# A Mamba block and a quantised feed-forward net on one core: three of eight C products on GpSimd, at other places, and another slack for the sums

## Chip, cores and metric

The kernel runs on one core of a Trainium2 chip. The metric is the device time of one launch in microseconds; the median of nine runs stands for the kernel. The engines are called by the profile's names: PE (matrix multiply), PEld (its weight load), DVE (vector), ACT (activation), POOL (GpSimd), SP (the queue that issues the DMAs).

## What is computed

Eight images of 384 channels and 1024 positions go through a Mamba-like block and an MLP, and then (five of the eight) through a feed-forward net with binarised weights and quantised activations. All is float32. The part that the change touches is the selective scan:

```
xz = t @ in_proj_w.T; xm, z = split(xz)
xc = silu(conv(xm, 3 taps))
dt, Bm, Cm = split(xc @ x_proj_w.T)
dt = softplus(dt @ dt_proj_w.T + dt_proj_b)
dA  = exp(einsum('bld,dn->bldn', dt, A))
dBu = einsum('bld,bln->bldn', dt * xc, Bm)
def step(hst, inp):
    dA_t, dBu_t, C_t = inp
    hst = dA_t * hst + dBu_t
    return hst, einsum('bdn,bn->bd', hst, C_t)
y = scan(step) + xc * D
y = y * silu(z)
t = y @ out_proj_w.T
t = gelu(t @ mlp_w1.T + mlp_b1) @ mlp_w2.T + mlp_b2
```

There are 768 inner channels d and 16 states n.

## The kernel before

**Stages.** `write_down` goes over the eight images b (called batches in the code). `s1` normalises, projects, convolves and makes dt, dt times xc, z and the rows of B and C, which go to DRAM. `s2` is the scan. `s3` is the output projection and the MLP. `ffn` is the quantised net for the first five images; `binarise` prepares its weights once, beside image 0. The matmuls of s1, s3 and ffn pass through `matmuls` (L444).

**The scan.** `scan` handles one image in 12 units. A unit has eight tiles: two tiles i (0 and 1) for each of four quads q (four states each). A tile is 128 partitions (32 channels times four states) by 1024 positions. In the first and the last image the work is done in halves of the positions, and a tile holds two pieces of 512. For one tile, `scan_tile` writes down these steps:

- ACT: da = exp(dt times A), into a PSUM buffer (L460; ring "da" of two buffers);
- POOL: u = dtx times B, into an SBUF buffer (L798; ring "u" of nine buffers);
- DVE: the scan over positions (L802), written into da, or into u where the tile is "on POOL";
- the product with C: on DVE, u = da times C (L819), or on POOL, u = u times C (L816);
- in the first half of the first and the last image also a copy of the last column as state, by ACT (L813) or POOL (L810).

`on_pool(i, q)` says which tiles have their product with C on POOL: now i = 1 with q = 1 and q = 3, two of eight.

When two quads are done (BATCH = 2: four tiles), one PE step `sums` adds the four states of all four tiles into the PSUM tile py (L729, 16 recorded matmuls); with it their four u buffers come free. After the unit's second step of sums DVE adds xc times D (L759), and POOL multiplies by z (L769, in the last image L765).

**What sets the order.** Every operation is first written down with an engine, a cost and its dependencies (`Plan.add`). `Plan.run` is a list scheduler: it runs a model of the five engines, picks the next operation for each by lane and image, and emits the instructions in that order. Each engine then works through its queue in order. Operations of lane 0 are the scan; DVE and POOL prefer operations of other lanes that are ready, PE prefers the sums (lane -1). What an operation uses of a ring is free again when its last user has ended in the model. SLACK is a time that is added to the end of the sums' inputs:

```
op.slack = SLACK if self.prio[0] < 0 else 0.0
```

and, for each operation `n` that follows an operation,

```
n.ready = max(n.ready, end + n.slack + (0.0 if n.engine == e != "SP" else SIGNAL))
```

(the attribute is the follower's own), so the sums are not planned before SLACK has passed after their last input. Where the model finds PE idle for more than 0.7 us, it emits "spare" matmuls (L375), whose result nobody uses. SP issues all loads and stores of the scan in the planned order: dt and dtx of a tile (L678), xc and z of a unit (L752), its result (L775), and the weights for PE (L423).

Of the kernel before, what the change touches and what calls it, by code (L numbers as in the profile page):

```python
# [53 lines left out]
POOL_TILES = True  # L54
# [21 lines left out]
IDLE = 0.7  # L76
EARLY = 2
PATIENCE = 0.0
SLACK = 1.6
LOAD_TABLE = 1.29  # L80


# [76 lines left out]
class Plan:  # L159
# [12 lines left out]
    def add(self, engine, cost, emit, r=(), w=(), claim=(), table=None, lock=False, size=0):  # L172
# [3 lines left out]
        op.next, op.ready, op.tiles = [], 0.0, []  # L176
        op.slack = SLACK if self.prio[0] < 0 else 0.0
        deps = set()
# [140 lines left out]
class Layer:  # L319
# [457 lines left out]

    def on_pool(self, i, q):

        return POOL_TILES and i == 1 and q % 2 == 1  # L780

    def scan_tile(self, hcs, cols, n, dt_r, dtx_r, bq, cq, state, half, on_pool):
        nc, add = self.nc, self.plan.add
        wide = len(cols)
# [411 lines left out]
```

## Time and profile before

| | |
|---|---|
| median of nine runs | 3402.45 us |
| lowest and highest | 3397.96 and 3407.19 us |
| the profiled execution | 3406.76 us, its span 3405.0 us |
| mean granted PE clock | 0.967 |
| products with C on DVE (L819) | 576 of 1222 ns |
| products with C on POOL (L816) | 192 of 2356 ns |
| products with B on POOL (L798) | 768 of 2362 ns |
| steps of sums (L729) | 3072 recorded matmuls, 380.3 us busy |

The page of the profile has the busy time of each engine, the chain of work that ended last (followed back from the last instruction, to what released each step), and groups of instructions. A group's line has the source line, the engine, the operation, its output and inputs, the shapes and the count; behind the first bar the busy time in us and the mean of one in ns; behind the second the idle time of the engine just before these instructions and what ended most of it. An answer on one line of the code lists who it waited for as "what: us in total, times". In a table of stretches each row has the stretch and its length, and then for each engine its busy time in it and the number of instructions.

### The profile page before, as it was taken

Reading aid. Unit: us, or ns where it says so; the run is one execution under the profiler, and the core shown is the slowest. Engines: PE = TensorE matmul, PEld = TensorE weight load, DVE = VectorE, ACT = ScalarE, POOL = GpSimd, SP = SyncE. Lnnn points to the kernel's source line nnn. Section 1 sums busy time; section 2 is a strip of 40 time slices with the busy share of each in tenths; the row PEclk is TensorE's granted clock in tenths of the full one; section 3 lists DMA queues with packets and bytes.
Section 4 is the critical chain, followed back from the end, with each engine's and each line's share of the span. In section 5 each row is a group of like instructions: output and inputs, shape, how many; then the busy total and the mean of one; then the engine's idle time right before and its main releaser. Section 6 shows DMA issues by size and latency. Waiting matters only on the chain.

```text
span 3405.0 us, 32501 instructions
## 1 busy us (share of the span) xinstructions
PE 3225.7 (95%) x10356; PEld 1334.8 (39%) x10356; DVE 2877.3 (85%) x2179; ACT 2017.0 (59%) x2278; POOL 2642.9 (78%) x1312
## 2 busy tenths in 40 slices
PE   8888898999899999899999999999999999999999
PEld 4333333344333334333344444344333444433334
DVE  3577798899897999899989989899887999988990
ACT  4677566566754556645565656666557546555551
POOL 1687776788698878799868789777888788888870
PEclk9988998999999999899999999999999999999999
DMA  6787857766687556966578676975668656666542
GB/s 192 250 287 225 253 166 228 239 192 217 226 284 230 194 185 231 298 225 221 176 257 271 197 260 222 305 219 188 239 227 280 216 196 219 225 201 209 172 136 75
DMA packets 369370, 751.77 MB, mean 221 GB/s; under 512 B 35376, under 2 KB 112688, under 8 KB 369200
## 3 DMA queue, kind: packets, MB, share of 16 engines
q1 hardware_dynamic: 367472, 749.60, 67.7%
q8 instruction: 83, 1.36, 0.2%
q14 instruction: 87, 0.71, 0.1%
q10 hardware_dynamic: 1728, 0.09, 0.0%
HBM read 569.21 MB, written 180.36 MB: 220 GB/s over the span
## 4 chain that ended last, share of the span: by engine, by line
PE 68%; DVE 10%; DMA 8%; ACT 8%; issue 3%; POOL 2%; SPq 1%; ACTq 0%; DVEq 0%; POOLq 0%
PE p_y L444 16%; PE p_o L444 11%; PE p_h L444 10%; PE py L729 7%; DVE da L802 6%; PE p_z L444 6%; PE p_out L444 5%; PE p_in L444 5%; ACT da L460 3%; ACT L460 2%; PE p_sum L473 2%; DVE u L819 2%; PE p_dt L628 1%; PE p_dbc L444 1%; PE spare L375 1%
## 5 line engine op out<-in xcount | busy, mean ns | idle before, releaser
L798 POOL TENSOR_TENSOR u<-dtx_r,bc 128x1024 f32<-128x1024 f32 x768 | 1794.8, 2362 | 378.9 <-PE py L729 326.9
L802 DVE TENSOR_TENSOR_SCAN da<-da,u 128x1024 f32<-128x1024 f32 (+1 forms) x576 | 1164.3, 2021 | 184.8 <-ACT da L460 132.9
L460 ACT ACTIVATE da<-dt_r,a_neg 128x1024 f32<-128x1024 f32 (+1 forms) x960 | 902.2, 945 | 702.4 <-DVE u L819 562.1
L819 DVE TENSOR_TENSOR u<-da,bc 128x1024 f32<-128x1024 f32 x576 | 703.6, 1222 | 18.4 <-ACT state L813 0.9
L816 POOL TENSOR_TENSOR u<-u,bc 128x1024 f32<-128x1024 f32 x192 | 452.4, 2356 | 116.5 <-DVE u L802 110.3
L444 PE MATMUL p_h<-t,w_b 128*128 128x512 f32 x1152 | 522.7, 607 | 19.1 <-DMA w_b<-in_mlp_w 10.4
L444 PE MATMUL p_o<-g,w 128*128 128x512 f32 x1152 | 513.0, 601 | 9.4 <-DMA w<-in_mlp_w 5.8
L802 DVE TENSOR_TENSOR_SCAN u<-da,u 128x1024 f32<-128x1024 f32 (+1 forms) x192 | 384.4, 2012 | 23.3 <-ACT da L460 19.4
L729 PE MATMUL py<-u,fold 128*32 128x512 f32 x3072 | 380.3, 610 | 5.4 <-POOL u L816 5.4
L444 PE MATMUL p_y<-gf,w_n 128*128 128x512 f32 x720 | 324.8, 606 | 25.3 <-ACT gf L460 21.0
L444 PEld LDWEIGHTS p_h<-t,w_b 128*128 128x128 f32 x1152 | 217.0, 193 | 313.3 <-issue 261.5
L444 PEld LDWEIGHTS p_o<-g,w 128*128 128x128 f32 x1152 | 217.1, 191 | 301.9 <-issue 284.8
L444 PE MATMUL p_y<-tn,w_b 128*128 128x512 f32 x720 | 328.0, 602 | 2.6 <-DVE tn L517 0.9
L460 ACT ACT_TABLE_LOAD x220 | 282.3, 1283 | 10.5 <-DVE xc L590 6.6
L444 PE MATMUL p_out<-yg,w 128*128 128x512 f32 x552 | 248.3, 602 | 8.7 <-ACT da L460 4.1
L444 PE MATMUL p_in<-t,w_f 128*128 128x512 f32 x504 | 234.6, 612 | 19.0 <-DMA w_f<-in_in_proj_w 14.4
L444 PE MATMUL p_z<-t,w_f 128*128 128x512 f32 x504 | 231.4, 607 | 8.3 <-ACT z L563 5.3
L444 PEld LDWEIGHTS p_y<-gf,w_n 128*128 128x128 f32 x720 | 136.8, 193 | 211.1 <-issue 177.7
L444 PEld LDWEIGHTS p_y<-tn,w_b 128*128 128x128 f32 x720 | 135.3, 192 | 180.8 <-issue 161.8
L802 DVE TENSOR_TENSOR_SCAN da<-da,state,u 128x512 f32<-128x512 f32 x144 | 185.0, 1284 | 23.3 <-ACT da L460 10.0
L590 DVE SCALAR_TENSOR_TENSOR xc<-p_in,conv_w,xc 128x511 f32<-128x511 f32 x192 | 141.4, 743 | 61.1 <-ACT halo L585 33.6
L729 PEld LDWEIGHTS py<-u,fold 128*32 128x32 f32 x3072 | 81.6, 110 | 273.1 <-issue 201.0
(100 smaller groups left out, 2759.0 us busy)
## 6 DMA issues: line engine op xcount, KB each, us to landing
dtx_r<-dtx_d SPq DMA_DIRECT2D x144, 512.0 KB, 5.4
dt_r<-dt_d SPq DMA_DIRECT2D x144, 512.0 KB, 5.6
w_b<-in_mlp_w SPq DMA_DIRECT2D x192, 192.0 KB, 2.6
w<-in_mlp_w SPq DMA_DIRECT2D x96, 384.0 KB, 3.4
w_f<-in_in_proj_w SPq DMA_DIRECT2D x168, 192.0 KB, 4.5
y_d<-y SPq DMA_DIRECT2D x120, 256.0 KB, 3.5
gf<-y_d SPq DMA_DIRECT2D x20, 1536.0 KB, 9.4
xc_d<-xc SPq DMA_DIRECT2D x32, 768.0 KB, 8.7
```

What stands on the lines that cost most here:

```text
L375: self.plan.fill = lambda: self.nc.tensor.matmul(self.plan.spare.real[:, : 2 * P], self.ones, self.ones.unsqueeze(1).to_broadcast([P, 2, P ...
L444: self.nc.tensor.matmul(p.real, w.real[:, w0 + k, :], t.real[:, k0 + k, :], start=start and k == 0, stop=stop and k == n - 1,)
L460: lambda: self.nc.scalar.activation(out(), in_(), func, **{k: v() if callable(v) else v for k, v in kw.items()}),
L473: nc.tensor.matmul(p_sum.real, self.ones, t.real[:, k, :], start=(k == 0), stop=(k == KC - 1))
L590: nc.vector.scalar_tensor_tensor(xc.real[:, m, s:], pm.real[:, : T - s], tap[2 - s], xc.real[:, m, s:], ALU.mult, ALU.add,)
L628: add("PE", MM / 2, lambda i=i, k=k, pd=pd, dbc=dbc, w=w: nc.tensor.matmul(pd.real, w.real[i : i + R, k % KC, :], dbc.real[i : i + R, :], ...
L729: nc.tensor.matmul(py.real[p0 : p0 + DQ, :], self.fold, hc, start=(q == 0), stop=(q == NQUAD - 1),)
L798: add("POOL", 2.36, lambda: nc.gpsimd.tensor_mul(u.real, dtx_r.real, spread(bq)), r=[dtx_r, bq], w=[u])
L802: add("DVE", 0.13 + n * 0.0021, lambda k=k, col=col: nc.vector.tensor_tensor_scan(to.real[:, k, :], da.real[:, k, :], u.real[:, k, :], sta ...
L816: add("POOL", 2.36, lambda: nc.gpsimd.tensor_mul(u.real, u.real, spread(cq)), r=[cq], w=[u])
L819: add("DVE", 1.21, lambda: nc.vector.tensor_mul(u.real, da.real, spread(cq)), r=[da, cq], w=[u])
```

## The change

```diff
-SLACK = 1.6
+SLACK = 0.8
...
     def on_pool(self, i, q):
 
-        return POOL_TILES and i == 1 and q % 2 == 1
+        return (i == 0 and q % 2 == 0) or (i == 1 and q == 0)
```

The product with C of three tiles of a unit is on POOL: i = 0 with q = 0 and q = 2, and i = 1 with q = 0. The tiles i = 1 with q = 1 and q = 3, which are the last of their four, go to DVE. So a unit's first four tiles have two products on POOL (the first two of the four), and its last four have one (the first of the four). The sums are planned from 0.8 us after their last input, in place of 1.6 us. Nothing else is edited; the scheduler plans all queues anew from this.

## The prediction

> **What bounds the kernel now.** I read the busy times first, then the chain that ended last, the groups of instructions, the waits, and the engines' busy time in stretches of 100 us.
>
> ```profile
> PE 3225.7 (95%) x10356; PEld 1334.8 (39%) x10356; DVE 2877.3 (85%) x2179; ACT 2017.0 (59%) x2278; POOL 2642.9 (78%) x1312
> ```
> ```profile
> PE 68%; DVE 10%; DMA 8%; ACT 8%; issue 3%; POOL 2%; SPq 1%; ACTq 0%; DVEq 0%; POOLq 0%
> ```
>
> PE is the main bound, with DVE close behind. The chain of waits runs over DVE for 10% of the span (340 us) and over POOL for 2%. What can still be won is what PE loses: 179 us idle (3405.0 - 3225.7), 98.8 us in "spare" matmuls, which the planner puts where it foresees an idle PE, and some 112 us of lowered clock ((1 - 0.967) x 3405). The groups give the prices:
>
> ```profile
> L798 POOL TENSOR_TENSOR u<-dtx_r,bc 128x1024 f32<-128x1024 f32 x768 | 1794.8, 2362 | 378.9 <-PE py L729 326.9
> L819 DVE TENSOR_TENSOR u<-da,bc 128x1024 f32<-128x1024 f32 x576 | 703.6, 1222 | 18.4 <-ACT state L813 0.9
> L816 POOL TENSOR_TENSOR u<-u,bc 128x1024 f32<-128x1024 f32 x192 | 452.4, 2356 | 116.5 <-DVE u L802 110.3
> L729 PE MATMUL py<-u,fold 128*32 128x512 f32 x3072 | 380.3, 610 | 5.4 <-POOL u L816 5.4
> ```
>
> L798 is the product with B, L819 and L816 the product with C on DVE and on POOL, L729 the sums over the states on PE. POOL idles 326.9 us because all nine u buffers are full and only the sums free one, and 110.3 us because a scan isn't finished. It is ahead of the scan, not behind it. PE itself idles only 5.4 us for the sums. The stretches (PE, PEld, DVE, ACT, POOL busy, then clock, DMA share, GB/s):
>
> ```profile
> 200.00:300.00 100.00, 86.31 (x248) 35.09 (x249) 75.18 (x76) 68.59 (x101) 89.65 (x64) 0.86 0.78 246
> ...
> 1500.00:1600.00 100.00, 98.60 (x310) 39.30 (x309) 90.20 (x64) 55.13 (x55) 96.89 (x48) 1.00 0.63 212
> ...
> 2000.00:2100.00 100.00, 100.00 (x340) 43.47 (x339) 92.84 (x66) 57.34 (x59) 94.19 (x47) 1.00 0.66 228
> ...
> 2700.00:2800.00 100.00, 99.79 (x370) 46.20 (x368) 99.35 (x77) 50.06 (x58) 78.88 (x37) 1.00 0.67 211
> ```
>
> From 2700 to 2800 DVE is full, and PE, though "busy", runs 15.7 us of spare matmuls (12.1 more from 2800 to 3000): DVE paces. From 1500 to 1600 and from 2000 to 2100 POOL is nearly full. The bound changes place.
>
> **What the Trainium skill says.** The "GPSIMD Engine Reference", section "Elementwise — side-by-side cycle accounting", puts a two-input elementwise operation there at about twice DVE's time (1.96 times). The trace agrees: 2356 to 1222 ns is 1.93. The same page, "Specifications", says that the two engines contend for SBUF where the DVE instruction has two SBUF inputs. L802 and L819 read one operand from PSUM (da), and L816 spreads only from 2336 to 2397 ns, so I add no contention. "Perfetto Trace Analysis", section "Identifying the Most-Contended Engine", holds matmul busy time to be a poor measure; the spare matmuls in the 2700 stretch show why.
>
> **The change part by part.** 96 units of eight tiles (eight batches of twelve units).
>
> *Product moved.* A third C product per unit goes to POOL: L816 from 192 to 288, L819 from 576 to 480. POOL gains 96 x 2.356 = 226.2 us (to 2869, 84%), DVE loses 96 x 1.222 = 117.3 (to 2760, 81%). 96 scans then write u in place of da, which costs the same (2280 against 2286 ns). Per unit of the present 33 us, DVE's load goes from 30.0 to 28.7 us and POOL's from 27.5 to 29.9 (busy time by 96): POOL takes DVE's place. In batch 0 and in the last one, 12 copies of the state move from ACT (158 ns) to POOL (190 ns): 2 us beside other work, nothing. No moved step issues a DMA.
>
> *Gain where DVE paces.* DVE loses 117.3 of 2877.3 us, 4.1%; of the 340 us in which it is on the chain that is **-14 us**. From 2700 to 3000 the chain shows PE's spare matmuls, so that this loss lies outside the 340: some nine units (three per 100 us) need 9 x 1.222 = 11 us less DVE, against 27.7 us of spare: **-11 us**. Next late there are PE's own matmuls.
>
> *The place in the batch.* Now the last tile of each batch of two quads has its product on POOL, behind the last scan. DVE's work up to it is 4 x 2.28 + 3 x 1.22 = 12.8 us, then 2.36 on POOL, then SLACK 1.6: the sums are planned 16.8 us after the batch's first scan. With the change the last product is DVE's: 4 x 2.28 + 2 x 1.22 + 0.8 = 12.4 us in a unit's first batch, 12.8 + 0.8 = 13.6 in its second. The u buffers come free 3.8 us earlier per batch, against a POOL wait for them of 326.9/192 = 1.7 us per batch. That makes room for POOL's 1.18 us more per batch; it gives no time itself, since POOL's waits lie off the chain: 0. If that room isn't there, it is the second rival.
>
> *SLACK 1.6 to 0.8* adds no instruction. It places 192 groups of sums 0.8 us nearer to their inputs in PE's order; behind a waiting group queue all PE matmuls. The waits at L729 are these:
>
> ```profile
>   DVE da L802: 33.0, 56
>   DVE u L819: 24.1, 38
>   POOL u L816: 13.4, 4
> ```
>
> They are waits of the weight load, hidden by running matmuls up to 5.4 of 70.5 us. If these 98 come 0.8 us sooner, that is 78 us of waits, and at the same share 78 x 5.4/70.5 = **+6 us**. The ends are 0 (the inputs come sooner by more than the order does) and +78 (nothing hides them).
>
> *POOL's queue.* Behind a C product on POOL wait B products, the gate product L769, xc times dt (L639) and the clip L1018; who waits for these is DVE's scan (57.4 us today) and SP's loads of dtx_r (107.0 us behind L798), with PE's weights behind them in SP's queue. The cover is the three dtx_r buffers and PE's small waits for DMA (14.4 us at most in a group). Where POOL has no idle time left the cover is gone: a unit more there needs 3 x 2.356 = 7.1 us per 100 us, so 1500 to 1600 goes to 103.96 and 2000 to 2100 to 101.26: **+5 us**. The upper end is taken up in the rival below. A da buffer comes free at the scan's end, 1.22 us sooner, but the tile after it also starts 1.22 us sooner: 0, with +-5, since DVE's 167.9 us of waiting for ACT show no finer split. The planner orders every queue anew; I allow +-10 us and take 0.
>
> Sum: -14 - 11 + 6 + 5 = **-14 us**. On the profiled execution's 3406.8 us that is 3393; it lies 4.3 us above the median of the nine runs, so the forecast for the median is 3402.45 - 14 = **3388 us**.
>
> **The rivals.** *More comes back.* PE's 390 us of losses hold more than the chain shows, and half of DVE's 117.3 us reaches the end: -58 + 6 = -52, 3350 us. For it speaks that DVE idles less than POOL in the later stretches (about 9.5 against 17 us per 100 from 1100 to 3300); against it, that PE is busy at 97% there, so DVE's relief can only shift PE's work. Chance 0.09.
>
> *PE holds the end.* DVE's relief only turns into DVE idle time, and the 6 us of SLACK cancel the rest: 3402 us. For it: 68% of the chain is PE, and the last 100 us are PE without a gap. Chance 0.15.
>
> *POOL becomes the pacing engine* (slower). With 29.9 us per unit it carries what DVE carries now, in a queue that holds products waiting for a scan. 13 of the stretches of 100 us have POOL at 85% or more. If 7.1 us per stretch were all lost there, that would be 92 us; half of it, less the 14 us that DVE gives back, is +32: 3434 us. It decides once POOL's idle time between 1100 and 3300 can't fall from 17 to 10 us per 100 without DVE waiting for L798. Against it: 326.9 us of POOL's idle time are the full u ring, which the new places shorten; for it, that the 2.36 us buy only 1.22. Chance 0.36.
>
> **How the numbers follow.** Forecast 0.40 at 3388, faster with the first rival: 0.49. Within 0.2% (6.8 us, about what a measurement of this kernel can tell from no change): 0.15. Slower: 0.36. The range reaches to both outer cases, 3345 to 3440; the forecast's own is 3365 to 3400.
>
> **What would show it.** Right: L816 x288 and L819 x480; POOL near 84%, DVE near 81%; POOL's wait at L798 for the sums well under 326.9 us; fewer spare matmuls between 2700 and 3000; PE's idle time before L729 under 12 us. Wrong: DVE's wait for L798 far above 57.4 us and POOL's share of the chain above 2% (POOL paces), or PE's idle before L729 at tens of us (SLACK).

## The result and the profile after

The changed kernel took 3387.93 us (median of 10 runs, 3377.52 to 3391.34) against 3406.39 us for the kernel before (32 runs): a ratio of 0.9945, with a 95% interval of 0.9934 to 0.9956. That is 18.5 us less, where 14 were forecast. The profiled execution's span fell by 17.6 us, from 3405.0 to 3387.4.

The lines of the page after that answer to those of before (busy times, chain, groups, the idle time before each group behind the second bar):

```profile
PE 3202.8 (95%) x10276; PEld 1316.7 (39%) x10276; DVE 2760.2 (81%) x2083; ACT 2024.5 (60%) x2273; POOL 2864.2 (85%) x1420
...
PE 67%; DMA 10%; POOL 7%; ACT 6%; DVE 5%; issue 3%; SPq 1%; ACTq 0%; POOLq 0%; DVEq 0%
...
L798 POOL TENSOR_TENSOR u<-dtx_r,bc 128x1024 f32<-128x1024 f32 x768 | 1790.4, 2364 | 83.1 <-DMA dtx_r<-dtx_d 63.3
...
L816 POOL TENSOR_TENSOR u<-u,bc 128x1024 f32<-128x1024 f32 x288 | 679.3, 2365 | 163.1 <-DVE u L802 131.8
...
L819 DVE TENSOR_TENSOR u<-da,bc 128x1024 f32<-128x1024 f32 x480 | 586.2, 1221 | 12.2
...
L729 PE MATMUL py<-u,fold 128*32 128x512 f32 x3072 | 388.1, 611 | 12.4 <-POOL u L816 10.1
```

POOL's wait for the sums, 326.9 us before, is no longer the first releaser at L798. From the answer on that line, first what POOL waited for, then who waited for it (us, times):

```profile
  PE py L729: 12.1, 5
```
```profile
  DVE da L802: 73.3, 19
  DVE u L802: 44.4, 13
```

DVE thus waits 117.7 us for products with B, against 57.4 before. POOL is busy for 221 us more, all of it in idle time that it had. DVE's share of the chain falls from 10 to 5%, and POOL's rises from 2 to 7%. The durations of one operation stay as they were.

How far the scan has come tells more than the total. The table gives, from the traces, the start of the DVE step that closes a unit (L759), in us from the span's start:

| closing step of unit | 12 | 24 | 60 | 96 (the last) |
|---|---|---|---|---|
| before | 622 | 1017 | 2180 | 3328 |
| after | 598 | 986 | 2150 | 3275 |

The scan ends 53 us sooner. Of these, 31 us come in the first two images and 23 in the last three. The end of the program moves by 18 us only. The chain of waits from 3230 us on shows why; first the kernel before, then the changed one (start, us, what):

```profile
3325.59 1.85 PE py L729 x16
3327.45 11.36 PE p_out L444 x26
3339.23 30.90 PE p_h L444 x72
3370.13 30.91 PE p_o L444 x72
```
```profile
3272.78 1.85 PE py L729 x16
3274.63 31.10 PE p_o L444 x72
3305.73 15.45 PE p_out L444 x36
3321.61 30.90 PE p_h L444 x72
3352.51 30.91 PE p_o L444 x72
```

Before, only the second half of the last image is left for PE after the last sums, some 78 us. In the changed kernel PE is behind by a further 31 us of p_o and 4 us of p_out, and 113 us follow. So the time is the scan's end plus the PE work that is left then. The second term took back 35 of the 53 us.

The two terms hang together: a scan that ends sooner leaves PE less time beside it, and more is left over unless PE loses less. Over the whole span PE's spare matmuls went from 98.8 to 78.6 us, its idle time from 179.3 to 184.6 us and its useful busy time (busy without spare matmuls) from 3126.9 to 3124.2 us. The 17.6 us are thus spare matmuls that fell away, and PE idles no less than before.

Where PE gained is seen in the stretches from 500 to 1100, 1100 to 2600 and 2600 to 3000 us, before and after (PE, PEld, DVE, ACT, POOL busy, clock, DMA share, GB/s):

```profile
500.00:1100.00 600.00, 547.80 (x1828) 227.82 (x1826) 521.61 (x385) 366.12 (x397) 477.83 (x232) 0.94 0.70 230
1100.00:2600.00 1500.00, 1457.94 (x4744) 596.01 (x4738) 1353.64 (x958) 906.00 (x926) 1233.14 (x594) 0.98 0.71 232
2600.00:3000.00 400.00, 394.24 (x1320) 170.63 (x1319) 364.06 (x264) 225.33 (x240) 341.81 (x160) 1.00 0.68 221
```
```profile
500.00:1100.00 600.00, 562.54 (x1843) 230.47 (x1842) 519.88 (x378) 373.49 (x402) 533.30 (x257) 0.96 0.72 236
1100.00:2600.00 1500.00, 1442.76 (x4705) 584.16 (x4705) 1304.57 (x917) 920.54 (x941) 1352.76 (x647) 0.98 0.72 236
2600.00:3000.00 400.00, 392.21 (x1302) 167.59 (x1301) 361.05 (x262) 229.29 (x254) 370.83 (x176) 0.99 0.66 213
```

The spare matmuls in these stretches were 31.2, 21.9 and 28.3 us before, and 20.0, 13.6 and 23.2 us after. PE's useful busy time therefore grew by 14.7 + 11.1 = 25.9 us from 500 to 1100, at a higher clock too. It fell by 15.2 - 8.3 = 6.9 us from 1100 to 2600, and grew by 3.1 us from 2600 to 3000. Early, PE's idle time fell from 52 to 37 us. It is spread over many waits, none of them over 7 us, so that a faster scan feeds PE there is argued and not shown. In the middle PE was already at 97%, and the scan's lead stayed at 30 us from unit 24 to unit 60. From 1100 to 2600 the chain of waits goes over POOL for 7.4% in the changed kernel (products with B 5.1%, with C 2.3%), where before it went over DVE's scan for 3.5%: there POOL has taken DVE's place.

### The profile page after: what moved, and what is told of

Same layout as the page of the kernel before. It is cut to its first block, busy times and chain, and to the rows that moved or that the text cites. A ratio compares the mean times of both kernels' runs of the same rounds, so it can differ in the third digit from the quotient of the medians.

```text
span 3387.4 us, 32416 instructions
## 1 busy us (share of the span) xinstructions
PE 3202.8 (95%) x10276; PEld 1316.7 (39%) x10276; DVE 2760.2 (81%) x2083; ACT 2024.5 (60%) x2273; POOL 2864.2 (85%) x1420
## 4 chain that ended last, share of the span: by engine, by line
PE 67%; DMA 10%; POOL 7%; ACT 6%; DVE 5%; issue 3%; SPq 1%; ACTq 0%; POOLq 0%; DVEq 0%
PE p_y L444 16%; PE p_o L444 12%; PE p_h L444 10%; PE py L729 7%; PE p_out L444 6%; PE p_z L444 5%; PE p_in L444 4%; POOL u L798 4%; DVE da L802 2%; DMA w_f<-in_in_proj_w 2%; ACT da L460 2%; PE p_dbc L444 2%; PE p_sum L473 1%; POOL u L816 1%; DMA dtx_r<-dtx_d 1%
## 5 line engine op out<-in xcount | busy, mean ns | idle before, releaser
L798 POOL TENSOR_TENSOR u<-dtx_r,bc 128x1024 f32<-128x1024 f32 x768 | 1790.4, 2364 | 83.1 <-DMA dtx_r<-dtx_d 63.3
L802 DVE TENSOR_TENSOR_SCAN da<-da,u 128x1024 f32<-128x1024 f32 (+1 forms) x480 | 969.9, 2021 | 161.4 <-POOL u L798 73.3
L816 POOL TENSOR_TENSOR u<-u,bc 128x1024 f32<-128x1024 f32 x288 | 679.3, 2365 | 163.1 <-DVE u L802 131.8
L802 DVE TENSOR_TENSOR_SCAN u<-da,u 128x1024 f32<-128x1024 f32 (+1 forms) x288 | 574.0, 2011 | 115.6 <-ACT da L460 61.8
L819 DVE TENSOR_TENSOR u<-da,bc 128x1024 f32<-128x1024 f32 x480 | 586.2, 1221 | 12.2
L444 PE MATMUL p_h<-t,w_b 128*128 128x512 f32 x1152 | 521.7, 606 | 26.9 <-DMA w_b<-in_mlp_w 14.1
L444 PE MATMUL p_o<-g,w 128*128 128x512 f32 x1152 | 506.1, 595 | 5.0 <-DMA w<-in_mlp_w 4.5
L729 PE MATMUL py<-u,fold 128*32 128x512 f32 x3072 | 388.1, 611 | 12.4 <-POOL u L816 10.1
L460 ACT ACTIVATE g<-p_h,v_mlp_b 128x512 f32<-128x512 f32 x192 | 128.1, 680 | 131.6 <-PE p_h L444 131.2
L729 PEld LDWEIGHTS py<-u,fold 128*32 128x32 f32 x3072 | 82.9, 110 | 280.4 <-issue 199.5
```

The lines of the kernel that those rows point to most:

```text
L444: self.nc.tensor.matmul(p.real, w.real[:, w0 + k, :], t.real[:, k0 + k, :], start=start and k == 0, stop=stop and k == n - 1,)
L460: lambda: self.nc.scalar.activation(out(), in_(), func, **{k: v() if callable(v) else v for k, v in kw.items()}),
L729: nc.tensor.matmul(py.real[p0 : p0 + DQ, :], self.fold, hc, start=(q == 0), stop=(q == NQUAD - 1),)
L798: add("POOL", 2.36, lambda: nc.gpsimd.tensor_mul(u.real, dtx_r.real, spread(bq)), r=[dtx_r, bq], w=[u])
L802: add("DVE", 0.13 + n * 0.0021, lambda k=k, col=col: nc.vector.tensor_tensor_scan(to.real[:, k, :], da.real[:, k, :], u.real[:, k, :], sta ...
L816: add("POOL", 2.36, lambda: nc.gpsimd.tensor_mul(u.real, u.real, spread(cq)), r=[cq], w=[u])
```

## The experiments

The theory was that DVE's relief, with room in the u ring, speeds up the scan. The rivals: SLACK alone does it; the places alone do it; the gain is one lucky order. Beside each group of runs the kernel before ran on the same chip, and ratios are to it. "Last sums" is the start of the last matmul of L729 in the run's trace, and the PE work left is the time from there to the end of the span. The scan's place in time comes from one trace per kernel.

### One part of the change at a time

The product's new places without the new SLACK:

```diff
-SLACK = 0.8
+SLACK = 1.6
```

> The three products on POOL at their new places, SLACK left at 1.6. Theory (the relief of DVE and the earlier last product are what counts): 3390 us, 0.995 of before, POOL's wait at L798 for the sums well below 326.9 us, some 60 us. Rival 'SLACK does it': 3406 us, no difference from before, and the wait for the sums stays above 200 us.

3394.26 us, ratio 0.9957 (0.9940 to 0.9974). POOL's wait for the sums is 35.9 us, and the last sums start at 3256 us. The product's move carries the gain without the new SLACK.

SLACK alone, in the kernel before:

```diff
-SLACK = 1.6
+SLACK = 0.8
```

> SLACK 0.8 alone, two products at the old places. Theory: 3403 us, within 0.2% of before; POOL waits at L798 for the sums some 250 us in place of 326.9, and DVE stays at 85%. Rival 'SLACK does it': 3390 us or less.

3471.17 us, ratio 1.0185 (1.0168 to 1.0203): slower than either expectation. The wait for the sums stays at 298.2 us, so SLACK alone doesn't make the gain. The last sums come late as well, at 3338 us, and 131 us of PE's work follow. The loss has a place: from 2100 to 2400 PE is busy for 254.3 us of 300, against 295.8 before, at a clock of 0.88 to 0.93. At 2139 us PE stands still for 10 us at L729, since a C product on POOL is late. Its scan had ended at 2134 us, but in POOL's queue it stood behind xc times dt (L639) and steps of the quantised net (L1091, L1099) until 2146 us:

```profile
PEld py L729 <- POOL u L816: 13.8, 4, 10.9
PE py L729 <- POOL u L816: 11.3, 2, 10.0
```

(waits from 2100 to 2300: us in total, times, longest). In this order PE is exposed to the product of the batch's last tile. That the smaller SLACK does it by itself is not shown: with the same last tiles on POOL and SLACK 1.0, the run with three late products below has 1.3 us of such waits. PE's idle time at L729 is 25.9 us in all, against 5.4 before: 20 of some 65 us that were lost. The rest stays open; in the same stretch the chain also goes over loads and stores (6.2% w_f, 4.4% yg_d, 4.2% yg, from 2100 to 2300).

Two products on POOL, at early places, with the new SLACK and with the old one:

```diff
-        return (i == 0 and q % 2 == 0) or (i == 1 and q == 0)
+        return i == 0 and q % 2 == 0
```

> Two products per unit on POOL as before, but at i = 0 with q = 0 and q = 2 (the first tile of each four), SLACK 0.8. Theory: without the third product DVE keeps its load; 3400 us, 0.998 of before, POOL's wait at L798 for the sums near 100 us. Rival 'the places do it': 3385 us or less, as fast as the changed kernel.

3425.39 us, ratio 1.0054 (1.0037 to 1.0071), slower than expected; last sums at 3295 us, wait for the sums 76.1 us.

> Two products on POOL at i = 0 with q = 0 and q = 2, SLACK 1.6 as before: the places alone. Theory: the scan gains part (last sums at 3285 to 3310 us, since POOL's wait for the sums falls below 120 us), the total stays near before, 3400 to 3425 us. Rival 'the places make the gain': 3390 us or less.

3413.05 us, ratio 1.0012 (1.0003 to 1.0021); last sums at 3305 us, wait for the sums 43.4 us. In both, the early places alone speed up the scan, by 32 and 22 us, and the total doesn't fall: 126 and 108 us of PE work are left at the end. How the places act is seen at L798: the u buffers come free sooner, POOL's product with B is there in time, and DVE's wait for it falls from 57.4 us to 32.6 and 14.1 us, though DVE has as much to do as before. POOL's idle time moves elsewhere: it now waits over 310 us for the scan at L816.

The third product at its early place, with the same SLACK, then brings the last sums forward by 21 us more (SLACK 0.8: 3295 to 3274) and by 49 us (SLACK 1.6: 3305 to 3256).

### More products, and other places for the third

Four products:

```diff
-        return (i == 0 and q % 2 == 0) or (i == 1 and q == 0)
+        return q % 2 == 0
```

> Four of eight products on POOL (both tiles of q = 0 and q = 2), SLACK 0.8. POOL gets another 96 x 2.356 = 226 us, 3090 us in all, 32.2 us per unit of 33. Theory (three is near the balance, POOL full beyond it): slower than before, about 3440 us, with DVE waiting for L798 for over 200 us. Rival 'DVE is still the bound and each product moved gains': 3370 us.

3416.46 us, ratio 1.0025 (1.0015 to 1.0035). POOL is 90% busy over the span and 99% from 2600 to 3000, and the answer on L798 says who waits for it:

```profile
who waited for it (us, times):
  DVE da L802: 204.4, 87
  DVE u L802: 64.6, 16
```

Those are 269 us, against 57.4 before and 117.7 in the changed kernel. The last sums start at 3343 us, 69 us later than with three. Here POOL does set the pace; the loss is smaller than expected, because only 72 us of PE work are left.

Three products, at late places:

```diff
-SLACK = 0.8
+SLACK = 1.0
...
-        return (i == 0 and q % 2 == 0) or (i == 1 and q == 0)
+        return (i == 1 and q % 2 == 1) or (i == 0 and q == 3)
```

> Three products on POOL at late places (i = 1 with q = 1 and q = 3, and i = 0 with q = 3), SLACK 1.0. Theory (the number of products on POOL sets the scan's pace, and the place of a product little): the last sums start at 3255 to 3290 us, as in the changed kernel (3274) and not as before (3327); the total is that plus the PE work left over, 3380 to 3420 us. Rival 'the early places make the gain': last sums after 3310 us and POOL waiting at L798 for the sums for over 200 us.

3425.14 us, ratio 1.0049 (1.0031 to 1.0067); last sums at 3322 us. That is against the theory as it stood. POOL waits 137.9 us for the sums, eleven times as long as in the changed kernel, though not the 200 us that the rival had named; DVE's wait for L798, 126.2 us, is much as there. So the number of products gave the scan its gain only where their places let the u ring turn faster. This is one order, with a SLACK of its own; but 3322 lies outside the 3256 to 3287 us that four values of SLACK give with the early places (below).

Three products, with one of them moved to the unit's second batch:

```diff
-SLACK = 0.8
+SLACK = 1.5
...
-        return (i == 0 and q % 2 == 0) or (i == 1 and q == 0)
+        return (i == 0 and q % 2 == 0) or (i == 1 and q == 2)
```

> Three products on POOL, the unit's second batch having two of them (i = 1 with q = 2 in place of q = 0), SLACK 1.5. Theory: last sums at 3255 to 3285 us and some 90 us left for PE, total 3360 to 3375 us, faster than the changed kernel by 0.4% or more. Rival 'the places make the gain, and those of the changed kernel are the better ones': 3388 us or more.

3341.15 us, ratio 0.9798 (0.9782 to 0.9814), the fastest of all and faster than expected. Its last sums start at 3249 us, a little sooner than expected and 25 us before those of the changed kernel, and 93 us are left for PE. DVE waits 68.5 us for L798, and PE's idle time before L729 rounds to nothing:

```profile
L729 PE MATMUL py<-u,fold 128*32 128x512 f32 x3072 | 375.3, 605 | 0.0
```

Both terms are smaller: the scan's end by 25 us and the work left by 20. From 100 to 3249 us PE has 16.8 us more useful busy time than in the changed kernel (2929.8 against 2913.0, spare matmuls taken off); the mean clock over the whole span is 0.975 in place of 0.972. What share the place, the SLACK and the order have in this one kernel was not taken apart.

### Other values of SLACK: how much is the order?

The kernel before with SLACK 1.5, and the changed kernel with 0.9 and 0.2:

> The kernel before with SLACK 1.5 in place of 1.6: no mechanism of any theory is changed by a tenth of a microsecond, only the planned order may come out otherwise. Theory: within 0.3% of before (3396 to 3417 us). Rival 'any new order moves the time by as much as the change did': 0.5% or more away from before, on either side.

3410.81 us, ratio 1.0003 (0.9988 to 1.0019), no difference; here the new order came out alike (last sums at 3332 us, 78 us left).

> The changed kernel with SLACK 0.9 in place of 0.8, a new order and nothing else. Theory (the gain is the product's and not this one order's): 3380 to 3396 us. Rival 'the gain is the luck of one order': 3400 us or more.

3478.58 us, ratio 1.0209 (1.0178 to 1.0240): what the rival had named. The scan is as fast as in the best orders (last sums at 3258 us), yet 212 us of PE work are left:

```profile
3258.92 20.80 PE p_h L444 x48
3279.72 30.90 PE p_o L444 x72
3310.62 15.45 PE p_out L444 x36
...
3326.50 30.90 PE p_h L444 x72
3357.40 30.90 PE p_o L444 x72
3388.30 15.45 PE p_out L444 x36
...
3404.18 30.90 PE p_h L444 x72
3435.09 30.91 PE p_o L444 x72
```

The whole MLP of the last image, and part of that of the image before it, are still to do. PE lost part of its time earlier: from 2735 to 2785, 30.05 of its 45.11 us busy are spare matmuls, while the chain of waits goes over loads and stores of the images' results (17% x from mid_d, 12% tn from mid_d, 5% yg_d, from 2720 to 2800). The spare matmuls alone in two stretches (PE, PEld, clock, DMA share, GB/s):

```profile
2735.00:2785.00 50.00, 30.05 (x134) 25.06 (x134) 0.97 0.77 234
2785.00:2835.00 50.00, 11.81 (x44) 8.79 (x44) 0.97 0.46 147
```

So a faster scan is no gain by itself.

> The changed kernel with SLACK 0.2. Theory (SLACK acts through the order alone, PE's waits for the sums stay small): last sums at 3265 to 3295 us, PE idle before L729 below 40 us, and a total of 3365 to 3385 us, since less of PE's work is left when the scan ends (90 us in place of 113). Rival 'less slack makes PE wait at the sums': over 60 us of PE idle before L729 and 3400 us or more.

3374.06 us, ratio 0.9889 (0.9872 to 0.9906): last sums at 3287 us, 88 us left, PE idle 2.7 us before L729. The least SLACK does not make PE wait. Taken together, values of SLACK from 0.2 to 1.6 give totals of 3374, 3388, 3479 and 3394 us with the same three products. PE's idle time before L729 goes up and down with them (2.7, 12.4, 26.7 and 10.6 us). SLACK acts through the planned order, and the order's spread is larger than the change's gain. The luck of an order is thus part of the result; the sooner scan (3256 to 3287 us in these four) is not.

### The scan without most of PE's work

```diff
     def matmuls(self, p, w, t, k0, n, start, stop, r, claim, w0=0):
+        n = 1
```

> The kernel before with each matmul chain of the projections and MLPs cut to its first matmul (of three or six), in the code and in the planner's cost. It leaves out part of each product's sum over channels, some 1750 us of PE work; scan, loads, DVE, ACT and POOL keep their instructions. Theory (the scan's pace comes from DVE, then POOL, and PE only hides it): PE no longer binds, DVE at 92% or more, about 3120 us. Rival 'the scan waits for latencies, not for an engine': DVE and POOL both stay under 88%.

> The changed kernel with the same cut (each chain of projection and MLP matmuls reduced to its first matmul). Theory (the change speeds up the scan's own pace, and PE's work eats most of it): 50 us or more faster than the same cut of the kernel before, since the sums of the last unit came 53 us sooner in the full kernel. Rival 'POOL's added 226 us pace the scan once PE is out of the way': as slow as the cut kernel before, or slower.

3381.54 us (0.9904 of before, 0.9868 to 0.9939) and 3345.19 us (0.9819; 0.9779 to 0.9858). Busy times of the cut kernel before:

```profile
PE 2710.0 (80%) x11056; PEld 1497.2 (44%) x11056; DVE 2875.6 (85%) x2179; ACT 2008.3 (59%) x2275; POOL 2645.7 (78%) x1312
```

```profile
L375 PE MATMUL spare<-ones 128*128 128x256 f32 x5250 | 1233.4, 387 | 33.9 <-ACT y L460 12.0
```

1233.4 us of that PE time are spare matmuls. PE's useful busy time fell from 3126.9 to 1476.6 us, and the time by only 0.96%, all of it PE work left at the end (42 us in place of 78): the last sums start at 3339 us, no sooner than before. The 3120 us and the 92% of the expectation were wrong; over the span DVE stays at 85% and POOL at 78%, as the rival had it. These are averages: from 2600 to 3000 DVE is 94% busy, so that DVE never paces the scan by being full is not shown. The waits inside the scan are long (DVE 206.6 us for ACT's da and 69.5 for u, POOL 183.2 for u buffers and 169.4 for scans); that these set the pace is read from the trace, and no run takes one of them away.

With the change the cut kernel is 36 us faster, less than the 50 expected, and all of it in the scan: the last sums start at 3303 in place of 3339 us, and 42 us are left in both. So the shortening is the scan's own, and POOL's added work doesn't undo it.

One caution: the cut also changes the order. It brings later images' projections forward (DMA share 0.85 from 100 to 500 us, 0.75 before). The scan of the second image ends 104 us later than in the full kernel (1121 against 1017 us), and the other 72 units take 2220 us in place of 2311. What PE's work costs the scan from stage to stage can't be told from this total.

## Why the prediction was right, step by step

**The sum and the time.** -14 us were forecast, -18.5 us measured; the median came out at the forecast's 3388 us because the 32 runs of before lie 4 us above the nine that it started from. The direction has its reason in the scan, which every order that was tried of these three products shortened. That the size fits is luck: the sum held neither the scan's 53 us nor the 35 us that PE's leftover work took back, and other values of SLACK with the same products gave from 3374 to 3479 us, the last of them slower than before.

**Product moved.** Right in every count: L816 x288, L819 x480; DVE 2760 and POOL 2864 us, against 2760 and 2869 forecast. No contention showed: L819 stays at 1221 ns and L816 at 2365. The Trainium skill ("Perfetto Trace Analysis", "Optimizing Scalar/DVE Operations") warns that moving work between GpSimd and DVE might not help, as they share an SBUF read port. Here the load itself moved at full value, and the runs above show what limited the use of it.

**Gain where DVE paces.** The -14 us from DVE's share of the chain point the right way, but at another size: of the 117 us that DVE was relieved of, the scan's end got 53, and the program's end 18. The -11 us from 2700 to 3000 are not borne out. Spare matmuls fell there from 27.7 to 18.0 us, but rose from 0.6 to 5.2 us in the 100 us before, and PE's useful time from 2600 to 3000 grew by 3.1 us only. The gain came from 500 to 1100 us (25.9 us of busy time), where the prediction had no term of its own.

**The place in the batch** was set at 0 and called the room for POOL. The room is there: 326.9 us of waiting became 12.1. For the total the 0 stands with two early products (ratio 1.0012 at the old SLACK), but its reason, that POOL's waits lie off the chain, fails for the scan: DVE's wait for POOL fell with them, and the last sums came at 3305 in place of 3327 us, while three late products hardly did as much (3322). The place is a cause of its own for the scan, and the third product needs it.

**SLACK.** PE's idle time before L729 went from 5.4 to 12.4 us, +7 where +6 was worked out, just above the 12 that the text had set as the sign. The fit is luck: with the old SLACK and the same products it is 10.6 us, with SLACK 0.2 it is 2.7, so that most of the 7 us doesn't come from SLACK. What it missed is the order: the +-10 us allowed for a new order are far too narrow. One value of SLACK more or less moved the time by 91 us (0.8 to 0.9).

**POOL's queue.** DVE's wait for L798 doubled, from 57.4 to 117.7 us, and POOL's share of the chain rose to 7%. The prediction had named both as signs of the slower rival. They came, and the kernel was faster, so they don't decide. The +5 us for the stretches without POOL's idle time were not seen apart; but from unit 24 to unit 60, where both lie, DVE's relief brought the scan nothing. With four products the rival is real.

**PE holds the end** was a rival, and it is half of the truth: the scan's 53 us became 18 through PE's leftover work. The prediction read PE's 68% of the chain as the main bound. The cut kernel corrects that: PE's work fits around a scan that ended no sooner when half of that work was gone, and the two meet at the end. The skill's "Identifying the Most-Contended Engine" (in "Perfetto Trace Analysis") advises to optimise the engine with the highest occupancy first, but holds matmul busy time to be no good measure of how near PE is to its limit, since matmuls are pipelined. The warning counts here, for a reason beside the page's: 1650 us less of PE's useful busy time were worth 27 us.

## What to carry to other kernels

Where a list scheduler lays independent work around a serial loop, read two numbers of each run: when the loop ends, and how much work of the fuller engine is left then. A change to the loop shows in the first; the total can go either way, and several orders have to be run before a gain of half a per cent is put down to the change. Work moved to an engine with idle time helps little if that idle time is a wait for a buffer: here the third product paid off together with places that free the u buffers sooner.

## What the runs showed of the hardware

- Mean durations hardly changed with POOL's load: L816 took 2356 ns at 78% busy, 2365 at 85% and 2364 at 90%; L798 2362, 2364 and 2361 ns; DVE's L819 1222, 1221 and 1222 ns.
- The mean granted clock was lower where PE was busy for less of the time, spare matmuls included. In the cut kernel before, PE was busy for 71% from 100 to 1100 us (156 us of it spare) at a mean clock of 0.82, and for 89% from 1600 to 3000 us (773 of 1242 us spare) at 0.96; the full kernel had 90% at 0.93 and 98% at 0.99 there. Over the span the cut kernels' clock was 0.897, against 0.967 and 0.972. No run varied the spare matmuls alone.
